# A perceiver block: the probabilities turned on VectorE, the mix of four heads in row quarters, PSUM banks in turn

## The chip, the cores and the metric

The kernel runs on one core of a Trainium2 chip. The metric is the device time of one execution in microseconds (us). Engines are TensorE (PE in the profile, its weight loads PEld), VectorE (DVE), ScalarE (ACT), GpSimd (POOL) and SyncE (SP), which only issues DMAs here. All data are 32-bit floats.

## The reference

Sixty-four sequences of 32 tokens, 256 wide, go through three residual layers: attention to a context, attention within the sequence, and a mixture of experts. The change touches the first.

```python
# xattn: 16 heads of 64; q [64, 32, 256], kv [64, 257, 128]
qh = (q @ Wq).reshape(B, N, 16, 64).transpose(0, 2, 1, 3)
kh = (kv @ Wk).reshape(B, M, 16, 64).transpose(0, 2, 1, 3)
vh = (kv @ Wv).reshape(B, M, 16, 64).transpose(0, 2, 1, 3)
attn = softmax(einsum("bhnd,bhmd->bhnm", qh, kh) * 64 ** -0.5)
out = einsum("bhnm,bhmd->bhnd", attn, vh).transpose(0, 2, 1, 3).reshape(B, N, 1024)
out = out @ Wo + bo
...
x = x + xattn(layernorm(x), ctx_512)      # ctx_512: [64, 257, 128]
x = x + attn(layernorm(x))                # 4 heads of 64, 32 tokens, rotary angles
x = x + ffn(layernorm(x))                 # 8 experts, the best 2 of each token
```

## The kernel before, in words

**Tiling.** A tile is 128 tokens, so four sequences; there are 16 tiles, and 64 sequences in the loop `for n, (t, b) in enumerate(seqs)`. The key and value weights are folded: the queries are multiplied by the key weights once (`cross_queries`, for two tiles at a time), and the scores are then products with the raw context; the mix of the raw context by the probabilities comes next (`cross_mix`), and the value and output weights after it (`cross_output`).

**One sequence.** `cross_probs` works in four groups of four heads, so that the 128 partitions are 4 heads x 32 tokens. For a group it makes the scores of 257 context rows (L315, one PSUM bank), the negated maximum on VectorE (L319), and the exponential with its sum on ScalarE (L320); after every second group VectorE takes the reciprocals (L325) and scales both groups' first 256 probabilities (L327). The 257th context row goes another way (`p_last`, `lastT`, `u_last`). `probs_transposed` turns the probabilities in two halves of 128 context rows: four TensorE transposes into one bank (L338) and one ScalarE copy (L342). `cross_mix` multiplies the two halves with the context's rows, two products of 128 rows by 512 columns (16 heads x 32 tokens) that add up in one bank (L348), and ScalarE copies it to `cT` (L351).

**Order.** The instruction order of TensorE and SP is the program's own; a scheduler orders the other engines. In the loop's pass `n`, the mix of sequence `n` and the scores of sequence `n + 1` are woven with steps of three more strands, which a table `steps` names for each pass: `near` and `far` are the rests of the last two tiles (`rest`: output of the cross attention, self attention, routing), and `ahead` is the queries of a pair of tiles to come. Before the change a pass is

```python
probs_transposed(t, b, 0, pr, pts)
step()
next(scores, None)
next(scores, None)
step()
probs_transposed(t, b, 1, pr, pts)
nc.vector.transpose(lastT[:, b, :], p_last[t % 2][b])
next(scores, None)
step()
next(scores, None)
step()
step()
cross_mix(t, b, pts, kvs[t][1], cT)
step()
```

**PSUM.** The eight banks stand in three rings: three for the scores (tag `s`), two for transposes (`t`), three for all else (`a`). A ring's next tile waits until the tile that it takes the place of has been read.

**Names in the profile.** L291 `pqh` and L270 `pq` are the queries (L270 on the two halves of TensorE's rows in turn), L298 the scaling that evicts `pqh`, L281 and L283 the copies that evict `pq`; L364 `pov` is the value product (two column halves), with L374 (VectorE) and L372 (ScalarE) as its two evictions, L377 and L381 the output product, L386 its residual add; L197 transposes for other stages and L198 evicts them, L396 is the self attention's q/k/v product, L399 adds its bias, L426 its scores (two row halves by four column strips), L442 its exponential, L451 its small transposes, L456 its mix; L483 and L527 belong to the routing, L183 to the layer norms (a power on GpSimd), L1076 is the transpose of `p_last`. L712 and L745 are the experts' products, L684 a VectorE transpose there. After the loop the experts run in blocks of 128 rows with weights that SP loads into three lanes.

Of the kernel before, what the change touches and what calls it, by code (L numbers as in the profile page):

```python
# [24 lines left out]
MC = 2  # L25
ML = MC * P
# [24 lines left out]
def block_kernel(  # L51
# [29 lines left out]
    ps = ctx.enter_context(tc.tile_pool(name="ps", bufs=3, space=PSUM))  # L81
# [37 lines left out]
    def load_context(t):  # L119
        kv = kvp.tile([P, W1LEN], FP, tag="kv", name=f"kv{t}")  # L120
        kvT = kv[:, : 4 * M].rearrange("p (b m) -> p b m", b=4)
        kvA = kv[:, 4 * M : 4 * M + 4 * ML].rearrange("p (b c d) -> p b c d", b=4, c=MC)
        load(kvT, ctx_t[:, 4 * t : 4 * t + 4, :])
        load(kvA, ctx_a[:, 4 * t : 4 * t + 4, :, :])
        return kvT, kvA
# [11 lines left out]
    load(xwo_sb, xwo.rearrange("(c p) k -> p c k", p=P))  # L137
    for t in range(2, 4):
        load_tokens(t)
# [30 lines left out]
    def bank(shape, name):  # L170
        return ps.tile([P] + shape, FP, tag="a", name=name)
# [17 lines left out]
    def transposed(dst, src, n, name, beside=False):  # L189


        if beside:
            pt = ps.tile([P, n, P], FP, tag="t", bufs=2, name=f"tr{name}")
        else:
            pt = bank([n, P], f"tr{name}")
        for k in range(n):
            nc.tensor.transpose(pt[:, k, :], src[:, k * P : (k + 1) * P], ident)  # L197
        nc.scalar.copy(dst, pt)  # L198
# [5 lines left out]
    def last_rows():  # L204
        v_last = wk.tile([P, XH // 2, NB], FP, tag="v_last", bufs=1, name="v_last")
        pv = bank([XH // 2, NB], "pv")
# [10 lines left out]
        for half in range(2):  # L217
            pu = [bank([2, D], f"pu{half}_{par}") for par in range(2)]
# [31 lines left out]
    def cross_queries(c):  # L250
# [5 lines left out]
        for j in range(2):  # L256
            transposed(xqT[:, :, j * P : (j + 1) * P], xns[j], 2, f"q{2 * c + j}")


        qh = wk.tile([P, XH // 2, 2 * P], FP, tag="qh", bufs=1, name=f"qh{c}")  # L260
# [3 lines left out]
        def of_heads(i):  # L264
            pq = [bank([2, 8, SEQ], f"pq{c}_{i}_{par}") for par in range(2)]
# [19 lines left out]
        for i in range(4):  # L285
            yield
            pq = bank([2, 2 * P], f"pqh{c}_{i}")
# [17 lines left out]
    def cross_probs(t, b, kvT):  # L305
# [6 lines left out]
        probs[t, b] = pr  # L312
        for g in range(4):
            s = ps.tile([P, M], FP, tag="s", name=f"s{t}_{b}_{g}")
# [8 lines left out]
            if g % 2:  # L323
                two = slice(g - 1, g + 1)
                nc.vector.reciprocal(inv[:, two], sums[:, two])  # L325
                for i in (g - 1, g):
                    nc.vector.tensor_scalar(  # L327
                        pr[:, i, :ML], pr[:, i, :ML], inv[:, i : i + 1], None, ALU.mult
                    )
# [5 lines left out]
    def probs_transposed(t, b, j, pr, pts):  # L335
        tp = ps.tile([P, 4 * P], FP, tag="t", bufs=2, name=f"tp{t}_{b}_{j}")
        for g in range(4):
            nc.tensor.transpose(  # L338
                tp[:, g * P : (g + 1) * P], pr[:, g, j * P : (j + 1) * P], ident
            )  # L340
        pt = ptp.tile([P, 4 * P], FP, tag=f"pt{j}", name=f"pt{t}_{b}_{j}")
        nc.scalar.copy(pt, tp)  # L342
        pts.append(pt)

    def cross_mix(t, b, pts, kvA, cT):
        pa = bank([4 * P], f"pa{t}_{b}")
        for j in range(MC):
            nc.tensor.matmul(  # L348
                pa, kvA[:, b, j, :], pts[j], start=(j == 0), stop=(j == MC - 1)
            )  # L350
        nc.scalar.copy(cT[:, :, b, :], pa.rearrange("p (h n) -> p h n", n=SEQ))  # L351

    def cross_output(t, cT, lastT, ut):
# [4 lines left out]
        for half in range(2):  # L358
            pv = bank([4, P], f"pov{t}_{half}")
# [16 lines left out]
        po = bank([D], f"po{t}")  # L376
# [3 lines left out]
        for m in range(XH // 2):  # L380
# [3 lines left out]
            if m == 3:  # L384
                yield
        nc.vector.tensor_tensor(xs[t], po, xb, ALU.add)  # L386

    def self_attention(t, xn):
        xaT = wk.tile([P, 2, P], FP, tag="xaT", name=f"xaT{t}")
        transposed(xaT, xn, 2, f"s{t}", t < NT - 2)  # L390
        yield
        qkv = wk.tile([P, 3 * D], FP, tag="qkv", name=f"qkv{t}")
        for lo, hi in ((0, 512), (512, 768)):
            pq = bank([hi - lo], f"pqkv{t}_{lo}")
# [20 lines left out]
        transposed(qkT, qkv, 4, f"qk{t}")  # L415
# [831 lines left out]
```

## Time and profile before

| what | value |
|---|---|
| median of 3 runs (lowest to highest) | 807.62 us (801.75 to 809.26) |
| the profiled execution: its time, its span | 802.53 us, 800.8 us |
| granted TensorE clock | 0.993 |
| PE / PEld busy | 771.7 / 604.5 us |
| VectorE / ScalarE / GpSimd busy | 503.1 / 365.3 / 152.4 us |
| moved by DMA | 64.17 MB, mean 80 GB/s |
| VectorE's scaling of the probabilities, L327 | 256 of 353 ns, 79.7 us |
| TensorE's transposes of them, L338 | 512 of 279 ns, 80.5 us busy |
| their evictions on ScalarE, L342 | 128 of 591 ns, 75.6 us |
| the mix, L348 | 256 instructions of 604 ns, 123.2 us busy |

Durations are those of single instructions, from start to modelled end; TensorE's instructions overlap, so a mean of 604 ns does not say that the next one starts 604 ns later. The distance between starts is read from the timeline. Each f32 product appears as two instructions.

### The profile page before, as it was taken

How to read it: one execution, taken by the hardware profiler on the slowest of the kernel's cores; microseconds unless marked ns; L12 is line 12 of the kernel's file. 1: busy time of each engine (PE TensorE's matmuls, PEld its weight loads, DVE VectorE, ACT ScalarE, POOL GpSimd, SP SyncE). 2: the span in 40 equal slices, each digit the busy share in tenths (PEclk: the TensorE clock that was granted, in tenths of full speed). 3: DMA queues.
4: the chain of work that ended last, by engine and by line, in shares of the span. 5: the costliest groups of instructions: out<-in, count | busy, mean ns of one | idle time of the engine just before them, and what ended most of it. 6: DMA issues, size and time to landing. Idle time of an engine off the chain costs nothing. (4 is left out here: it accounts for less than half of the span.)

```text
span 800.8 us, 15293 instructions
## 1 busy us (share of the span) xinstructions
PE 771.7 (96%) x5146; PEld 604.5 (75%) x5146; DVE 503.1 (63%) x2084; ACT 365.3 (46%) x1052; POOL 152.4 (19%) x214
## 2 busy tenths in 40 slices
PE   8899999999999999999999999999999899999994
PEld 7576677677767777777767777676678799999994
DVE  4657666766686676677677766768665633554442
ACT  3564555555465555546554555555434222212220
POOL 3001011120211111111111111121124412332332
PEclk9999999999999999999999999999999999999997
DMA  9440102021120202021110202020351396458432
GB/s 309 142 111 2 67 11 68 11 89 27 53 73 18 67 11 80 11 69 50 50 60 18 68 11 67 10 78 15 119 203 34 80 398 180 54 110 251 58 45 28
DMA packets 44258, 64.17 MB, mean 80 GB/s; under 512 B 19408, under 2 KB 35152, under 8 KB 42640
## 3 DMA queue, kind: packets, MB, share of 16 engines
q1 hardware_dynamic: 37648, 54.08, 20.8%
q0 software_dynamic: 6528, 9.06, 6.2%
q8 instruction: 43, 0.70, 0.4%
q14 instruction: 39, 0.32, 0.1%
HBM read 87.54 MB, written 13.16 MB: 126 GB/s over the span
## 5 line engine op out<-in xcount | busy, mean ns | idle before, releaser
L320 ACT ACTIVATE pr<-s,nmx 128x257 f32<-128x257 f32 x256 | 122.2, 481 | 111.8 <-DVE nmx L319 100.5
L319 DVE TENSOR_REDUCE nmx<-s 128x1 f32<-128x257 f32 x256 | 105.4, 420 | 71.0 <-PE s L315 70.4
L315 PE MATMUL s<-kv,q 128*128 128x257 f32 x512 | 143.1, 388 | 1.9 <-ACT pr L320 1.9
L348 PE MATMUL pa<-pt,kv 128*128 128x512 f32 x256 | 123.2, 604 | 5.0 <-ACT ov L372 4.9
L315 PEld LDWEIGHTS s<-kv,q 128*128 128x128 f32 x512 | 89.3, 193 | 16.7 <-ACT pr L320 3.2
L338 PEld LDWEIGHTS tp<-ident,pr 128*128 128x128 f32 x512 | 61.8, 144 | 30.6 <-issue 15.7
L338 PE MATMUL tp<-ident,pr 128*128 128x128 f32 x512 | 80.5, 279 | 1.6 <-DVE pr L327 1.6
L327 DVE TENSOR_SCALAR pr<-pr,inv 128x256 f32<-128x256 f32 x256 | 79.7, 353 | 3.4
L351 ACT COPY cT<-pa 128x512 f32<-128x512 f32 x64 | 37.5, 586 | 91.4 <-PE pa L348 91.4
L342 ACT COPY pt<-tp 128x512 f32<-128x512 f32 x128 | 75.6, 591 | 4.5 <-PE tp L338 3.5
L348 PEld LDWEIGHTS pa<-pt,kv 128*128 128x128 f32 x256 | 46.1, 190 | 39.4 <-issue 26.6
L752 POOL DMA_INDIRECT out_x<-y_late,to_late x28 | 43.5, 1555 | 104.0 <-DMA out_x<-y_late,to_late 39.0
L291 PE MATMUL pqh<-xqT,xwq_sb 128*128 128x256 f32 x256 | 60.8, 381 | 0.8 <-ACT xqT L198 0.8
L381 PE MATMUL po<-xwo_sb,ov 128*128 128x256 f32 x256 | 60.6, 379 | 0.0
L381 PEld LDWEIGHTS po<-xwo_sb,ov 128*128 128x128 f32 x256 | 48.6, 190 | 6.6
L291 PEld LDWEIGHTS pqh<-xqT,xwq_sb 128*128 128x128 f32 x256 | 47.3, 190 | 7.9 <-ACT xqT L198 1.5
L320 ACT ACTIVATION_READ_ACCUMULATOR pr<-s,nmx 128x1 f32 x256 | 52.1, 203 | 0.0
L325 DVE RECIPROCAL inv<-sums 128x2 f32<-128x2 f32 x128 | 20.8, 162 | 46.7 <-ACT pr L320 45.8
L728 ACT ACTIVATE sa_late<-pa_late,lane 128x128 f32<-128x128 f32 x72 | 20.6, 369 | 63.6 <-PE pa_late L712 63.6
L555 POOL TENSOR_SCALAR carried<-seen,is_last 128x8 f32<-128x8 f32 x15 | 5.3, 353 | 218.6 <-DVE seen L550 218.6
L539 POOL DMA_INDIRECT routed<-xr,rslots x32 | 33.0, 1032 | 59.2 <-DMA routed<-xr,rslots 22.0
L396 PE MATMUL pqkv<-awqkv_sb,xaT 128*128 128x512 f32 (+1 forms) x128 | 43.9, 486 | 0.0
(275 smaller groups left out, 1270.8 us busy)
## 6 DMA issues: line engine op xcount, KB each, us to landing
lane<-in_wall SPq DMA_DIRECT2D x24, 1028.0 KB
lane<-in_wall SPq DMA_DIRECT2D x24, 640.0 KB
lane2a<-in_wall SPq DMA_DIRECT2D x10, 1028.0 KB
kv<-in_ctx_t SPq DMA_DIRECT2D x16, 514.0 KB
kv<-in_ctx_a SPq DMA_DIRECT2D x16, 512.0 KB
lane2b<-in_wall SPq DMA_DIRECT2D x10, 640.0 KB
xg_late<-routed SPq DMA_DIRECT2D x80, 32.0 KB
x<-in_x SPq DMA_DIRECT2D x16, 128.0 KB
```

The costliest lines, as they stand in the source:

```text
L291: nc.tensor.matmul(pq[:, mm, :], xwq_sb[:, k, m * P : (m + 1) * P], xqT[:, k, :], start=(k == 0), stop=(k == 1),)
L315: nc.tensor.matmul(s, qb[:, g * P : (g + 1) * P], kvT[:, b, :], start=True, stop=True)
L319: nc.vector.tensor_reduce(nmx, s, AX.X, ALU.max, negate=True)
L320: nc.scalar.activation(pr[:, g, :], s, AF.Exp, bias=nmx, accum_out=sums[:, g : g + 1])
L327: nc.vector.tensor_scalar(pr[:, i, :ML], pr[:, i, :ML], inv[:, i : i + 1], None, ALU.mult)
L338: nc.tensor.transpose(tp[:, g * P : (g + 1) * P], pr[:, g, j * P : (j + 1) * P], ident)
L342: nc.scalar.copy(pt, tp)
L348: nc.tensor.matmul(pa, kvA[:, b, j, :], pts[j], start=(j == 0), stop=(j == MC - 1))
L351: nc.scalar.copy(cT[:, :, b, :], pa.rearrange("p (h n) -> p h n", n=SEQ))
L381: nc.tensor.matmul(po, ov[:, m, :], xwo_sb[:, m, :], start=False, stop=(m == XH // 2 - 1))
L396: nc.tensor.matmul(pq, xaT[:, k, :], awqkv_sb[:, k, lo:hi], start=(k == 0), stop=(k == 1))
L752: nc.gpsimd.indirect_dma_start(out=out[:, :], out_offset=bass.IndirectOffsetOnAxis(ap=self.to[:, b : b + 1], axis=0), in_=y, in_offset=Non ...
```

## The change

- The scaling of the probabilities moves from VectorE to ScalarE. After every second group VectorE turns the two groups' 256 columns in squares of 32 x 32 (`prT`); TensorE's transposes and their ScalarE copies go.
- A square's transpose stays within its 32 partitions, so that head `h` of each group has its probabilities, turned, in partitions `32 h` to `32 h + 31`. The mix is therefore 8 chunks of 32 context rows x 4 heads of a group: 32 products of 32 rows by 128 columns (4 groups x 32 tokens), each head in its quarter of TensorE's rows and in its bank. One ScalarE copy empties the four banks.
- Each quarter needs the context's rows in its own partitions: the rows of a sequence are loaded four times (`load_values`, three buffers, asked for two sequences ahead), where a tile's were loaded once. The transposed context (`kvT`) keeps its load.
- The eight banks are one tile, and each use takes the bank, or the row of four, whose last use is longest ago; banks that stay open over several steps are held.
- To make room, the rotary tables' small tiles lie in a tile of the routing, the third lane in that of the queries, `v_last` in that of `xqT`, and `sa` and `g` of the experts share one tile. The host lays `ctx_a` out by chunks of 32.

```diff
-MC = 2
-ML = MC * P
+MC = 8
+ML = MC * SEQ
...
-    ps = ctx.enter_context(tc.tile_pool(name="ps", bufs=3, space=PSUM))
+    psum = ctx.enter_context(tc.tile_pool(name="ps", bufs=1, space=PSUM))
+    psum = psum.tile([P, 8, 512], FP, name="psum")
...
     def load_context(t):
-        kv = kvp.tile([P, W1LEN], FP, tag="kv", name=f"kv{t}")
-        kvT = kv[:, : 4 * M].rearrange("p (b m) -> p b m", b=4)
-        kvA = kv[:, 4 * M : 4 * M + 4 * ML].rearrange("p (b c d) -> p b c d", b=4, c=MC)
+        kvT = kvp.tile([P, 4, M], FP, tag="kvT", name=f"kvT{t}")
         load(kvT, ctx_t[:, 4 * t : 4 * t + 4, :])
-        load(kvA, ctx_a[:, 4 * t : 4 * t + 4, :, :])
-        return kvT, kvA
+        return kvT
+
+    def load_values(n):
+
+        kvA = kvp.tile([P, MC, KVD], FP, tag="kvA", bufs=3, name=f"kvA{n}")
+        for h in range(4):
+            load(kvA[h * SEQ : (h + 1) * SEQ, :, :], ctx_a[:, n, :, :])
+        values.append(kvA)
...
     load(xwo_sb, xwo.rearrange("(c p) k -> p c k", p=P))
+    values = []
+    for n in range(2):
+        load_values(n)
...
-    def bank(shape, name):
-        return ps.tile([P] + shape, FP, tag="a", name=name)
+    taken, held = [0] * 8, set()
+
+    def banks(n):
+
+        at = min(
+            (i for i in range(9 - n) if held.isdisjoint(range(i, i + n))),
+            key=lambda i: max(taken[i : i + n]),
+        )
+        taken[at : at + n] = [max(taken) + 1] * n
+        return at
...
+    def bank(shape):
+        return view(banks(1), shape)
+
+    def hold():
+        at = banks(1)
+        held.add(at)
+        return at
...
         pr = pp.tile([P, 4, M], FP, tag="pr", name=f"pr{t}_{b}")
-        probs[t, b] = pr
+        prT = ptp.tile([P, MC, 4, SEQ], FP, tag="pt", name=f"prT{t}_{b}")
+        probs[t, b] = prT
         for g in range(4):
-            s = ps.tile([P, M], FP, tag="s", name=f"s{t}_{b}_{g}")
+            s = bank([M])
...
                 for i in (g - 1, g):
-                    nc.vector.tensor_scalar(
-                        pr[:, i, :ML], pr[:, i, :ML], inv[:, i : i + 1], None, ALU.mult
-                    )
+                    nc.scalar.mul(pr[:, i, :ML], pr[:, i, :ML], inv[:, i : i + 1])
+
+                nc.vector.transpose(
+                    prT[:, :, two, :], pr[:, two, :ML].rearrange("p g (c m) -> p c g m", c=MC)
+                )
...
-    def probs_transposed(t, b, j, pr, pts):
-        tp = ps.tile([P, 4 * P], FP, tag="t", bufs=2, name=f"tp{t}_{b}_{j}")
-        for g in range(4):
-            nc.tensor.transpose(
-                tp[:, g * P : (g + 1) * P], pr[:, g, j * P : (j + 1) * P], ident
-            )
-        pt = ptp.tile([P, 4 * P], FP, tag=f"pt{j}", name=f"pt{t}_{b}_{j}")
-        nc.scalar.copy(pt, tp)
-        pts.append(pt)
-
-    def cross_mix(t, b, pts, kvA, cT):
-        pa = bank([4 * P], f"pa{t}_{b}")
-        for j in range(MC):
-            nc.tensor.matmul(
-                pa, kvA[:, b, j, :], pts[j], start=(j == 0), stop=(j == MC - 1)
-            )
-        nc.scalar.copy(cT[:, :, b, :], pa.rearrange("p (h n) -> p h n", n=SEQ))
+    def cross_mix(n, prT, kvA, cT):
+
+
+        at = banks(4)
+        for c in range(MC):
+            for h in range(4):
+                r = slice(h * SEQ, (h + 1) * SEQ)
+                nc.tensor.matmul(
+                    psum[:, at + h, :P],
+                    kvA[r, c, :],
+                    prT[r, c, :, :].rearrange("p g n -> p (g n)"),
+                    start=(c == 0),
+                    stop=(c == MC - 1),
+                )
+        nc.scalar.copy(
+            cT[:, :, n % 4, :].rearrange("p (g h) n -> p h g n", h=4),
+            psum[:, at : at + 4, :P].rearrange("p h (g n) -> p h g n", n=SEQ),
+        )
...
-        pr, pts = probs.pop((t, b)), []
-        probs_transposed(t, b, 0, pr, pts)
+            scores = cross_probs(t1, b1, kvs[t1])
+        if n + 2 < len(seqs):
+            load_values(n + 2)
         step()
         next(scores, None)
+        step()
         next(scores, None)
+        nc.vector.transpose(lastT[:, b, :], p_last[t % 2][b])
         step()
-        probs_transposed(t, b, 1, pr, pts)
-        nc.vector.transpose(lastT[:, b, :], p_last[t % 2][b])
         next(scores, None)
         step()
         next(scores, None)
         step()
-        step()
-        cross_mix(t, b, pts, kvs[t][1], cT)
+        cross_mix(n, probs.pop((t, b)), values[n], cT)
         step()
```

## The prediction

> **What bounds the kernel now.** I read the page's engine shares first, then a table by stage, then who waited for whom, then the timeline of TensorE in the loop.
>
> ```profile
> PE 771.7 (96%) x5146; PEld 604.5 (75%) x5146; DVE 503.1 (63%) x2084; ACT 365.3 (46%) x1052; POOL 152.4 (19%) x214
> ```
>
> TensorE's share is an average, so the loop over the sequences has to be looked at by itself (columns: window, PE, PEld, DVE, ACT, POOL busy with counts, granted clock, DMA share, GB/s):
>
> ```profile
> 200.00:300.00 100.00, 98.88 (x656) 72.32 (x656) 70.38 (x290) 54.96 (x158) 16.86 (x27) 1.00 0.14 45
> 300.00:400.00 100.00, 98.88 (x648) 72.80 (x647) 69.12 (x281) 54.03 (x157) 16.15 (x26) 1.00 0.16 52
> ```
>
> TensorE is busy 98.9% at full clock; VectorE has 30% idle, ScalarE 45%, the DMA engines 85%. Who held TensorE up, in the whole span (total us, times, longest):
>
> ```profile
> PE pa L348 <- ACT ov L372: 4.9, 13, 0.4
> PE s L315 <- ACT pr L320: 1.9, 3, 1.0
> PE tp L338 <- DVE pr L327: 1.6, 1, 1.6
> ```
>
> So the loop lasts as long as TensorE's own stream. The first mix products (L348) of sequences 4 and 56 start at 61.5 and 526.5 us: 465/52 = 8.94 us a sequence. What a group costs is the distance from its start to the next group's (start, busy, group):
>
> ```profile
> 291.76 0.60 PE L315 MATMUL s<-kv,q 128*128 128x257 f32 x2
> 292.29 1.14 PE L270 MATMUL pq<-qh,xwk_sb 64*128 64x256 f32 x8
> 293.36 0.70 PE L315 MATMUL s<-kv,q 128*128 128x257 f32 x2
> ...
> 302.71 1.88 PE L348 MATMUL pa<-pt,kv 128*128 128x512 f32 x4
> 304.42 0.28 PE L527 MATMUL pk<-rfed,before_all 128*128 128x8 f32 x2
> ...
> 305.07 1.03 PE L315 MATMUL s<-kv,q 128*128 128x257 f32 x4
> 305.94 0.60 PE L197 MATMUL trqk<-ident,qkv 128*128 128x128 f32 x4
> 306.38 0.60 PE L338 MATMUL tp<-ident,pr 128*128 128x128 f32 x4
> ...
> 310.29 0.38 PE L426 MATMUL pss<-qkT 64*32 64x32 f32 x32
> 311.05 1.13 PE L348 MATMUL pa<-pt,kv 128*128 128x512 f32 x2 [0.37 <-ACT ov L372]
> ```
>
> An f32 product is two instructions, a transpose is one. 128 columns step at 0.11 us (306.38 - 305.94 over 4), 257 at 0.217, 512 at 0.43. The reader should see L270: eight instructions of 256 columns on two row halves take 1.07, where one after the other would be 8 x 0.217 = 1.74. The halves run side by side.
>
> **Part by part: TensorE.** Removed for each sequence: 8 transposes x 0.11 = 0.88, and the mix, 304.42 - 302.71 = 1.71. Together 2.59, over 64 sequences 165.8. Added: 32 products of 32 rows x 128 columns, 64 instructions, four quarters taking turns. If four run at once that is 16 steps x 0.11 = 1.76. Entering and leaving a split array costs too: L270 takes 1.07 where four steps are 0.87 (0.20), and the score product ahead of it takes 0.53 and not 0.435 (0.10). So 2.06, over 64 131.8. No row has four row quarters. The bounds are 1.76 (no switch) and 64 x 0.11 + 0.30 = 7.34 (one at a time); two at a time is 32 x 0.11 + 0.30 = 3.82. The nearest rows are L270 (a full two at a time on two halves) and L426 (two halves by four column strips: 32 instructions of 32 columns start within 0.38 - 0.20 = 0.18 us, where single file at 0.027 would be 0.83, so more than four run at once). I take 2.06. Net -33.9.
>
> The first page rule against this: the Trainium skill ("TensorE: Matmul & The Clock Gate", section "Measured speedup vs the span model") measured four row quarters at 3.07 times one, not 4. By it the mix would be an estimated 7.04/3.07 + 0.30 = 2.59, nothing would be won on the products, and the sum below would end at about 811. The trace has pairs only, and those lose nothing but the switch.
>
> The second: the same page ("The mechanism") says that a weight load overlaps running products only where the row group differs. Each quarter here loads new weights for every product. But the full-array mix above loads 0.19 us of weights (L348's PEld row) for each product in a 0.43 step with no gap, on the same rows, so the trace disagrees. With L270's load of 0.186 in the open in each step the mix would be about 5.0, and the sum about 967.
>
> **VectorE and ScalarE.** (line, engine, op, shapes, count, busy us, mean ns, idle before)
>
> ```profile
> L327 DVE TENSOR_SCALAR pr<-pr,inv 128x256 f32<-128x256 f32 x256 | 79.7, 353 | 3.4
> L342 ACT COPY pt<-tp 128x512 f32<-128x512 f32 x128 | 75.6, 591 | 4.5 <-PE tp L338 3.5 <-ACT cT L351 0.2
> ...
> L1076 DVE STREAM_TRANSPOSE lastT<-p_last 128x32 f32<-128x32 f32 x64 | 13.0, 203 | 0.2
> L684 DVE STREAM_TRANSPOSE bxT_late<-xg_late 128x256 f32<-128x256 f32 x20 | 8.7, 435 | 0.0
> L442 ACT ACTIVATE apr<-sc,zero 128x128 f32<-128x128 f32 x16 | 6.4, 401 | 10.8 <-DVE sc L434 10.8
> ```
>
> VectorE loses 256 scalings (79.7) and gets 128 transposes of 512 elements. From 32 to 256 elements costs 232 ns, 1.04 a column, so 435 + 265 = 0.70 each, 89.6: +10. ScalarE loses 75.6 of evictions and gets 256 scalings of 128x256 in SBUF; the rows around are 0.371 (L198's copy, 256 columns), 0.401 (L442, the one that reads SBUF) and 0.481 (L320). I take 0.40: 102, or +27. Per sequence that is +0.15 and +0.41 against idle of 2.8 and 4.1: nothing by the sums. Both orders are fixed queues, though, so the waits matter more.
>
> What is new there: reciprocal (VectorE), two scalings (ScalarE), transpose (VectorE) is a round trip, and VectorE queues later maxima, and with them the exponentials that free score banks, behind the transpose. The mix needs the transposed probabilities one whole sequence later, so it does not wait for them. It waits for banks. In the changed kernel's order the four banks of a mix were mostly last used three or more groups back. In one of four sequences (the one after which a tile ends) the newest of them is the third score's, with one score product (0.435) in between. From the end of the second score: 0.20 to land, max 0.42, exponential with sum 0.63, reciprocal 0.16 = 1.41. In one tile of two, the q/k/v product (2.57) stands between second and third score, so the mix could start at 2.57 + 0.87 = 3.44; VectorE adds the bias (starts at 1.91 when its product has landed, to 2.52), transposes (the scalings ended at 2.26) to about 3.14, adds the other bias to 3.50, takes the third max to 3.92; the exponential ends at about 4.45. Stall 1.0. In the other tile 1.71 stands there, and the mix could start at 2.58; ScalarE's order is scalings to 2.3, eviction of the queries (0.60) to 2.9, third exponential to 3.4. Stall 0.85. Mean 0.93 x 16 = +15. Bounds: 0 if the scheduler's slack is larger than I count, and 45 if every mix waits 0.7, one transpose.
>
> **Banks, memory, loads.** Banks in turn put the mix on banks other than the second L372 eviction's: the 4.9 goes, and with the transposes the 1.6 goes: -6.5. The values come four times over, 512 KB a sequence and not 128, 25 MB more, by four DMAs on SP, asked for two sequences (some 17 us) ahead. The page's first slice moves 309 GB/s, so 512 KB take 1.7 us; SP has only stores and later loads behind that wait. Cost nothing; if this cover went, 1.7 x 64 = 109 would be the most. The first values now come behind the output weights, some 4.5 MB into the stream or 15 us at that rate, still ahead of the first mix (30.1 us). The rotary tables' and third lane's new places cost nothing while their old owner is done well before: the queries' tile is last used some eight sequences earlier. The expert stage keeps its products and two held banks: nothing.
>
> **Sum.** -33.9 + 15 - 6.5 = -25.4 on the profiled execution's 802.5 us (span 800.8): 777.1. That execution stands 0.6% under the median, 807.62, of runs from 801.75 to 809.26. I forecast 777.
>
> **Rivals.**
> - VectorE's queue becomes the bound (the slower side). In the loop:
>
> ```profile
> DVE nmx L319 <- PE s L315: 48.4, 57, 2.1
> DVE inv L325 <- ACT pr L320: 34.3, 57, 0.8
> ```
>
> from 100 to 500 us, 44.7 sequences. Waiting for scores is slack; waiting for exponentials (0.77 a sequence), for GpSimd's powers (0.32) and the small exponential (0.09) is not. VectorE's busy 6.18 + 0.15 + 1.18 = 7.51; two round trips of 0.80 with nothing queued between make 9.11, 0.17 above 8.94: +11, 813. It decides from 1.43 us unfilled on; against it, the order puts a bias add, eviction or residual add in most of the gaps, and half filled leaves 8.3. Chance 0.13.
> - The quarters run two at a time or with loads in the open: 3.82 adds 1.76 x 64 = 113 to the sum: about 890. For it, no row shows four; against it L426. Chance 0.09.
> - Half way: stalls at all mixes (45, not 15) give 807, no change. For it, VectorE is 70% busy and in order. Chance 0.15.
> - No stall at all: 762. For it, the trace before has almost none. Chance 0.10.
> - Forecast: 0.53.
>
> **How the numbers follow.** 1% is what a measurement here tells from no change. Faster (below some 799): forecast, no stall and a part of the half-way case, 0.68. Same: most of the rest of the half-way case, 0.12. Slower: VectorE's queue with its upper neighbours, and the quarters, 0.20. Range: from 757, a little under no stall, to 815, just past VectorE's queue; the quarters' case is left out. The forecast's own range is 762 to 792.
>
> **What would show it.** The mix group at 2.0 to 2.1 us from its start to the next group's (3.8 says two at a time); VectorE's transposes at 0.70; the scalings at 0.40; mix starts 8.5 us apart; TensorE's waits naming the mix behind the third exponential about 15 us in total and in every fourth sequence; VectorE waiting for scores still, though less. I am wrong if VectorE no longer waits for scores, or if the mix takes over 2.6.

## The result

The changed kernel takes 810.41 us (median of 15 runs), the kernel before 804.69 (15 runs): 1.0074 times as long, 95% interval 1.005 to 1.0099. So it is a little slower, where 777 us were forecast. The profiled execution has a span of 809.0 us (before 800.8).

The page's engine shares of the changed kernel:

```profile
PE 766.7 (95%) x8474; PEld 640.0 (79%) x8474; DVE 507.7 (63%) x1956; ACT 406.2 (50%) x1180; POOL 151.6 (19%) x214
```

Two hundred microseconds of its loop by stage (window, PE, PEld, DVE, ACT, POOL busy, granted clock, DMA share, GB/s):

```profile
200.00:300.00 100.00, 98.07 (x1229) 78.35 (x1229) 71.33 (x268) 61.64 (x178) 16.88 (x27) 1.00 0.29 89
300.00:400.00 100.00, 98.07 (x1219) 78.43 (x1218) 69.99 (x257) 61.44 (x179) 16.12 (x26) 1.00 0.32 95
```

TensorE still looks full. A busy share does not show what happened inside: TensorE's groups got shorter, and its waits longer. The groups of the new parts (busy us, mean ns of one, idle time before them):

```profile
L375 PE MATMUL psum<-prT,kvA 32*128 32x128 f32 x4096 | 157.7, 282 | 9.9 <-ACT pr L351 4.8 <-DMA bn_bc<-in_bias_n 1.1 <-DVE qkv L435 1.0
L375 PEld LDWEIGHTS psum<-prT,kvA 32*128 32x128 f32 x4096 | 138.2, 188 | 30.4 <-issue 10.3 <-ACT pr L351 8.5 <-ACT q L311 2.5
L358 ACT ACTIVATE pr<-pr,inv 128x256 f32<-128x256 f32 x256 | 115.7, 502 | 39.5 <-DVE inv L356 37.7 <-issue 1.2
L360 DVE STREAM_TRANSPOSE prT<-pr 128x512 f32<-128x512 f32 x128 | 89.7, 701 | 30.1 <-ACT pr L358 30.0
```

The mix (L375) is 64 instructions in one group. Undisturbed, the first and the last of them start 1.80 us apart (16 steps of four quarters, 0.21 us from the first step to the second and 0.11 from then on), and the next group starts at 2.0. By place in the eight sequences of two tiles (sequences 8 to 55, means in us; the stall is what the distance from first to last start has over 1.80):

| place | 0 | 1 | 2 | 3 | 4 | 5 | 6 | 7 |
|---|---|---|---|---|---|---|---|---|
| mix to next mix, before | 9.92 | 8.58 | 9.93 | 9.00 | 9.92 | 8.12 | 8.22 | 8.24 |
| mix to next mix, after | 9.91 | 8.29 | 9.51 | 9.01 | 9.81 | 8.29 | 8.10 | 8.91 |
| stall inside the mix, after | 0.45 | 0 | 0.21 | 0.74 | 0.34 | 0 | 0.53 | 1.54 |

The stalls come to 3.81 in eight sequences, 30 us in 64. Places 0 and 4 have 0.79 of the 3.81; there the profile names nothing that the mix waits for. TensorE's timeline at the worst place (a place 7, sequence 31):

```profile
301.87 1.03 PE L346 MATMUL psum<-kvT,q 128*128 128x257 f32 x4
302.83 0.49 PE L375 MATMUL psum<-prT,kvA 32*128 32x128 f32 x4
303.51 0.48 PE L375 MATMUL psum<-prT,kvA 32*128 32x128 f32 x2 [0.19 <-DVE qkv L435]
304.44 2.05 PE L375 MATMUL psum<-prT,kvA 32*128 32x128 f32 x58 [0.45 <-ACT pr L351]
306.42 0.39 PE L563 MATMUL psum<-rfed,before_all 128*128 128x8 f32 x2
```

Four of its 64 instructions run, then it waits for a bank that the q/k/v addition (L435) empties, then for one that the third score's exponential (L351) empties: 3.59 us to the next group and not 2.0. VectorE's timeline says why that exponential is late:

```profile
301.30 0.17 DVE L356 RECIPROCAL inv<-sums 128x2 f32<-128x2 f32 x1 [0.76 <-ACT pr L351]
301.38 0.67 DVE L435 TENSOR_TENSOR qkv<-psum,abqkv_bc 128x512 f32<-128x512 f32 x1
302.44 0.71 DVE L360 STREAM_TRANSPOSE prT<-pr 128x512 f32<-128x512 f32 x1 [0.39 <-ACT pr L358]
303.07 0.39 DVE L435 TENSOR_TENSOR qkv<-psum,abqkv_bc 128x256 f32<-128x256 f32 x1
303.38 0.41 DVE L350 TENSOR_REDUCE nmx<-psum 128x1 f32<-128x257 f32 x1
```

The third maximum (L350) stands behind a transpose that waits for ScalarE's scalings. So far the prediction's picture holds. What it does not say is how much of this belongs to the waiting transpose, and how much to the bank that the mix picked.

Where the profiled 8.2 us went: the first mix starts at 27.1 us (before 30.1), the last at 582.7 (580.8), and from there to the end it is 226.3 us (220.0): -3.0, +4.9, +6.3. Over sequences 4 to 56 a sequence takes 8.98 us, before 8.94, and the forecast said 8.5. The loop kept nothing of the saving, and the stage behind it lost more.

### The profile page after: what moved, and what is told of

It is laid out like the page before. It is cut to its first block, busy times and chain, and to the rows that moved or that the text cites. A ratio compares the mean times of both kernels' runs of the same rounds, so it can differ in the third digit from the quotient of the medians.

```text
span 809.0 us, 22230 instructions
## 1 busy us (share of the span) xinstructions
PE 766.7 (95%) x8474; PEld 640.0 (79%) x8474; DVE 507.7 (63%) x1956; ACT 406.2 (50%) x1180; POOL 151.6 (19%) x214
## 5 line engine op out<-in xcount | busy, mean ns | idle before, releaser
L351 ACT ACTIVATE pr<-psum,nmx 128x257 f32<-128x257 f32 x256 | 120.8, 475 | 106.2 <-DVE nmx L350 105.7
L375 PE MATMUL psum<-prT,kvA 32*128 32x128 f32 x4096 | 157.7, 282 | 9.9 <-ACT pr L351 4.8
L375 PEld LDWEIGHTS psum<-prT,kvA 32*128 32x128 f32 x4096 | 138.2, 188 | 30.4 <-issue 10.3
L346 PE MATMUL psum<-kvT,q 128*128 128x257 f32 x512 | 150.3, 394 | 1.0 <-ACT q L311 0.8
L358 ACT ACTIVATE pr<-pr,inv 128x256 f32<-128x256 f32 x256 | 115.7, 502 | 39.5 <-DVE inv L356 37.7
L350 DVE TENSOR_REDUCE nmx<-psum 128x1 f32<-128x257 f32 x256 | 103.0, 413 | 42.3 <-PE psum L346 41.2
L360 DVE STREAM_TRANSPOSE prT<-pr 128x512 f32<-128x512 f32 x128 | 89.7, 701 | 30.1 <-ACT pr L358 30.0
L346 PEld LDWEIGHTS psum<-kvT,q 128*128 128x128 f32 x512 | 87.5, 190 | 22.6 <-issue 9.6
L747 PE MATMUL psum<-bxT_late,lane 128*128 128x128 f32 x576 | 69.1, 275 | 1.2 <-DMA lane<-in_wall 1.2
L747 PEld LDWEIGHTS psum<-bxT_late,lane 128*128 128x128 f32 x576 | 68.1, 192 | 2.3 <-ACT bxT_late L717 1.3
L351 ACT ACTIVATION_READ_ACCUMULATOR pr<-psum,nmx 128x1 f32 x256 | 50.5, 197 | 0.0
L575 POOL DMA_INDIRECT routed<-xr,rslots x32 | 33.0, 1030 | 48.4 <-DVE nmx L350 17.8
```

The source lines that it names most:

```text
L346: nc.tensor.matmul(s, qb[:, g * P : (g + 1) * P], kvT[:, b, :], start=True, stop=True)
L350: nc.vector.tensor_reduce(nmx, s, AX.X, ALU.max, negate=True)
L351: nc.scalar.activation(pr[:, g, :], s, AF.Exp, bias=nmx, accum_out=sums[:, g : g + 1])
L358: nc.scalar.mul(pr[:, i, :ML], pr[:, i, :ML], inv[:, i : i + 1])
L360: nc.vector.transpose(prT[:, :, two, :], pr[:, two, :ML].rearrange("p g (c m) -> p c g m", c=MC))
L375: nc.tensor.matmul(psum[:, at + h, :P], kvA[r, c, :], prT[r, c, :, :].rearrange("p g n -> p (g n)"), start=(c == 0), stop=(c == MC - 1),)
```

## The experiments

All ratios are against the kernel before, with 95% intervals. "First to last mix" is from the profile, to tell the loop from the stage behind it.

**The scaling back on VectorE.**

```diff
-                    nc.scalar.mul(pr[:, i, :ML], pr[:, i, :ML], inv[:, i : i + 1])
+                    nc.vector.tensor_scalar(
+                        pr[:, i, :ML], pr[:, i, :ML], inv[:, i : i + 1], None, ALU.mult
+                    )
```

> The scaling of the probabilities goes back to VectorE, all else stays as changed. Theory A (the round trip from VectorE to ScalarE and back sits in VectorE's fixed order, makes the third maximum and ScalarE's evictions late, and the mixes wait for their banks): the wait of VectorE for the scalings (19.7 us from 100 to 500 us) goes, but two scalings of some 0.27 us each stand in its place ahead of the same third maximum, about as long as the two on ScalarE (0.91) less the hop; so little changes, 800 to 815 us. Rival B (VectorE's load as such is the bound of the loop): 4 x 0.27 = 1.1 us more a sequence, 64 x 1.1 = 70, about 870 us at the most and over 830 us at the least.

Measured 831.57 us, 1.0355 (1.0326 to 1.0384). 21 us above the changed kernel: too much for theory A. It lies at the lower edge of what rival B allowed (over 830), with a third of its 70. It is not spread evenly: at place 7 it is 11.23 us from mix to next mix, 2.32 more than in the changed kernel, and over all eight places 3.07 more. So VectorE's work isn't the bound everywhere, but where it is late already, more of it is paid.

**Half of the mix left out.**

```diff
-        for c in range(MC):
+        for c in range(MC // 2):
...
-                    stop=(c == MC - 1),
+                    stop=(c == MC // 2 - 1),
```

> The mix takes only the first four of its eight chunks of context rows, so half of the mix is left out; loads, transposes and scalings stay. It asks whether TensorE's stream is still what the loop lasts as long as. Theory A (TensorE's stream with waits inside it): eight steps of 0.11 us less a sequence, 64 x 0.88 = 56, so about 755 us, or some 770 us if part of it turns into longer waits for banks. Rival B (VectorE, ScalarE or a chain through them sets the pace of a sequence): the shorter mix is filled by waits, 795 to 810 us.

Measured 788.79 us, 0.9838 (0.9804 to 0.9873). The last mix starts at 565.1 us, 17.6 earlier, for 56 us of products left out. Neither theory as stated: TensorE's stream still matters, but less than a third of a saving gets through. At place 7 the halved mix still takes 3.11 us where it could take 0.90.

**Scalings and transposes in the next pass.** They are taken out of the groups' loop, kept for the next pass and pinned there (`keep_in_program_order`, here `pin`: behind what its engine was given before).

```diff
+        turn = turns.pop((t, b))
         step()
         next(scores, None)
+        scaled(turn, 0)            # pin(ScalarE: both scalings of a pair)
         step()
         next(scores, None)
         nc.vector.transpose(lastT[:, b, :], p_last[t % 2][b])
+        turned(turn, 0)            # pin(VectorE: the pair's transpose)
+        scaled(turn, 2)
         step()
         next(scores, None)
+        turned(turn, 2)
```

> The scalings and the transposes of a sequence are put off into the next pass, and pinned there: the first pair's scalings behind the first exponential of the next sequence on ScalarE and its transpose behind the second maximum on VectorE, the second pair's a group later. The same work, but nobody waits for a round trip any more: reciprocals are long done, scalings stand a group ahead of their transpose, and the mix is still half a pass away. Theory A: VectorE's waits for the scalings (19.7 us) go, the third maxima come earlier, and of the 29 us that mixes stand in the middle most go: 780 to 790 us. Rival B (the load of VectorE and ScalarE, or what TensorE pays for entering and leaving the split array, is the cause): no more than 5 us either way, 805 to 815 us.

A miss: 834.89 us, 1.0383 (1.0344 to 1.0421). Who waited for whom from 100 to 500 us:

```profile
PEld psum L388 <- DVE prT L376: 28.7, 32, 1.8
DVE prT L376 <- ACT pr L369: 23.3, 33, 1.2
```

The mixes (L388 here) now wait for the transposes (L376 here) themselves. The edit gave away the lead of nearly a whole sequence that the changed kernel has, and so tested something else.

**Banks 4 to 7 for the mix alone.**

```diff
+        if apart[0] and n == 4:
+            return 4
...
-            (i for i in range(9 - n) if held.isdisjoint(range(i, i + n))),
+            (i for i in range((4 if apart[0] else 8) + 1 - n) if held.isdisjoint(range(i, i + n))),
```

> While the loop runs (up to its last four passes), the mix has banks 4 to 7 for itself, and all other groups take turns in banks 0 to 3. A mix then waits only for the copy of the mix before, some 7 us back. Theory A in its narrow form (the mix's four banks are what waits, and nothing else is late): the 29 us of stalls inside the mixes go and a ring of four is deep enough for the rest, about 782 us. Theory A in its wide form (the maxima and exponentials are late, whoever waits for them): the waits move to the scores and to the products of the other strands, which now find their bank after four groups instead of some eight, 800 to 830 us. Rival B (loads, supply of instructions or engine load): no change, 805 to 815 us.

Measured 825.91 us, 1.0286 (1.0258 to 1.0315). Every mix now takes 1.80 us from first to last start, so with banks of its own it has no stall left. That would fit waits for banks at every place; for places 0 and 4 the run with three sequences' values, below, shows something else at work. And the loop is longer (9.22 us a sequence): the other groups wait instead in their ring of four. The wide form of theory A.

**One group earlier** (the edit is against the run with the next pass). The first pair's scalings stand at the head of the pass, its transpose behind the first maximum.

```diff
+        scaled(turn, 0)
         step()
         next(scores, None)
-        scaled(turn, 0)
+        turned(turn, 0)
+        scaled(turn, 2)
         step()
         next(scores, None)
+        turned(turn, 2)
         nc.vector.transpose(lastT[:, b, :], p_last[t % 2][b])
-        turned(turn, 0)
-        scaled(turn, 2)
         step()
         next(scores, None)
-        turned(turn, 2)
```

> As the run before with scalings and transposes in the next pass, but one group earlier each: the first pair's scalings at the head of the pass, its transpose behind the first maximum, the second pair's scalings behind the first exponential, its transpose behind the second maximum. There the mixes had turned to wait for the transposes (VectorE's second transpose was 28.7 us of TensorE's waits from 100 to 500 us). Theory A (the round trip inside a pass makes the third maximum late, and the mixes wait for banks): neither wait is left, VectorE's waits for scalings are under 5 us, and the loop comes to some 8.5 us a sequence: 780 to 790 us. Rival B (load): the lead gained is spent on other waits, and it stays at 805 to 830 us.

Measured 811.39 us, 1.0100 (1.0068 to 1.0132): no gain in time, against theory A. Sequences 4 to 56 take 8.83 us each, 0.15 less than in the changed kernel or 7.8 us together, but from mix 56 to the last mix it is 66.0 us and not 56.7: the last mix alone waits 5.4 us for its transposes, which stand behind a tile's routing here. So the total says little about the loop. In the loop the mixes at places 3 and 7 still stall, 0.84 and 1.02 us, though VectorE waits for no scaling there any more. So the waiting transpose is not what holds the mix.

**The scalings left out.**

```diff
-                for i in (g - 1, g):
-                    nc.scalar.mul(pr[:, i, :ML], pr[:, i, :ML], inv[:, i : i + 1])
```

> The scalings are left out (the mix gets unnormalised probabilities), all else as changed; a transpose then waits for its exponentials alone. ScalarE loses 4 x 0.41 = 1.64 us a sequence, and the way from the second exponential of a pair to the end of the transpose gets shorter by 0.16 for the reciprocal and 0.91 for the scalings. Theory A: the stalls inside the mixes (0.46 us a sequence) fall to a third or less and the waits ahead of other groups go too: 775 to 787 us. Rival B with ScalarE's load as the bound would give the same sign. Rival C (what TensorE pays for switching, the supply of its many instructions, or the order of its own stream costs the gain): nothing changes, 805 to 815 us.

Measured 815.75 us, 1.0144 (1.0091 to 1.0196). The unnormalised values send the tokens to other experts, and behind the last mix it takes 245.2 us, so only the loop can be read: 8.85 us a sequence, stalls of 0.73 and 1.27 at places 3 and 7. Even with no scaling in the kernel the stalls stay. Theory A as I had it falls here.

**The kernel before, with its scalings on ScalarE.**

```diff
-                    nc.vector.tensor_scalar(
-                        pr[:, i, :ML], pr[:, i, :ML], inv[:, i : i + 1], None, ALU.mult
-                    )
+                    nc.scalar.mul(pr[:, i, :ML], pr[:, i, :ML], inv[:, i : i + 1])
```

> The kernel before with one part alone: the 256 scalings on ScalarE in place of VectorE; TensorE's transposes, their copies, the three rings of banks and the loads stay. VectorE loses 4 x 0.27 = 1.1 us a sequence, ScalarE gains 4 x 0.41 = 1.64. Theory A (it is the round trip together with VectorE's transpose that hurts): without a VectorE transpose nothing on VectorE waits for the scalings but the products with the 257th column do not need them either, TensorE's transposes come a sequence later, so no change: 798 to 808 us. Rival B (ScalarE's share of evictions and exponentials is late as soon as scalings stand ahead of them): the score banks come free later, up to 0.9 us once or twice a sequence, 820 us and more.

Measured 823.08 us, 1.0239 (1.0183 to 1.0296): rival B. In the kernel before, with its three rings, this one part of the change costs some 19 us by itself. From mix to mix, 2.54 of the 2.75 us that eight sequences lose stand between the last mix of a tile and the first of the next. ScalarE's and TensorE's timelines where a tile begins:

```profile
317.90 0.93 ACT L327 ACTIVATE pr<-pr,inv 128x256 f32<-128x256 f32 x2
318.70 0.66 ACT L198 COPY xqT<-trq 128x256 f32<-128x256 f32 x2
319.14 1.09 PE L362 MATMUL pov<-cT,xwv_sb 128*64 128x128 f32 x16 [0.41 <-ACT xqT L198]
320.06 0.91 ACT L327 ACTIVATE pr<-pr,inv 128x256 f32<-128x256 f32 x2 [0.23 <-DVE inv L325]
320.87 0.56 ACT L370 COPY ov<-pov 128x512 f32<-128x512 f32 x1
321.18 1.10 PE L346 MATMUL pa<-pt,kv 128*128 128x512 f32 x2 [0.63 <-PE pss L424]
```

Two scalings stand ahead of the copy of `xqT`, and the value product waits 0.41 us for its bank; two more stand ahead of the copy of `ov`, and the mix starts 0.63 us late. The profile names L424 as its releaser, which had long been done. ScalarE is far from full, but it takes its instructions one after another in their order, and here 0.9 us of work that nobody waits for yet stands ahead of an eviction for which TensorE waits.

**A held bank counts as used when it is let go.**

```diff
-        held.remove(at)
+        release(at)                # held.remove(at); taken[at] = max(taken) + 1
...
-            held.difference_update(self.banks.pop(b))
+            release(*self.banks.pop(b))
```

> The changed kernel with one line of its turn of the banks changed: a bank that is held over several steps counts as used last when it is let go, not when it was taken. As changed, the next group takes just such a bank as the one longest unused and waits for its eviction: in the profile after, TensorE waits 1.70 and 1.52 us for the experts' gated product behind the loop, where the kernel before has no such wait. Expected: those two waits (3.2 us) go, and in the loop the bank of the output product is no longer taken at once after its release; 804 to 808 us. Rival (the 6.3 us behind the last mix come from VectorE's order and late gathers): no change, 808 to 812 us.

Measured 809.57 us, 1.0076 (1.0053 to 1.0099). From the last mix to the end it takes 225.0 us and not 226.3. In the changed kernel TensorE's waits behind the loop include these two:

```profile
PE psum L226 <- DVE sag_early L769: 1.7, 1, 1.7
PE psum L611 <- DVE sag_early L769: 1.5, 1, 1.5
```

Both are gone with the edit, but the experts' second product waits in their place (1.5 us for the same gated product), a wait that the kernel before has too. Those 6.3 us are for the most part something else.

**The row of four set aside ahead of the mix.** The alternatives so far changed when banks come free. This one changes only which are taken. As changed, the mix must find four neighbours when it comes. At places 3 and 7 every such row holds the third score's bank, which was used two groups back.

```diff
+            if not kept and 9 <= p < 60:      # p: mixes so far
+                if singles[p % 8] - since[1] <= ahead_of_mix[p % 4]:   # (4, 2, 2, 2)
+                    kept.append(oldest_row())
...
-            (i for i in range(9 - n) if held.isdisjoint(range(i, i + n))),
+            (i for i in range(8) if i not in held and not (kept and kept[0] <= i < kept[0] + 4)),
```

> The changed kernel with the same instructions in the same order on TensorE, and only other banks: a few groups ahead of each mix (four in the sequence that begins a tile, two in the others) the row of four whose use is longest ago is set aside, and the groups until the mix take turns in the other four. As changed, a row of four neighbours must be found when the mix comes, and in the last sequence of each tile it always holds the third score's bank, used two groups back; now the newest bank of a row was used four or more groups back. Theory D (the earlier theory A has fallen, since neither putting the scalings off nor leaving them out took the stalls away: it is the row of four banks next to each other that makes the mix wait for the newest score's exponential): the stalls of those sequences (0.74 and 1.54 us) go, 8 x 2.28 = 18 us, and some 6 more in the first sequences of tiles: 786 to 793 us. Theory E (the strands' own chains through VectorE and ScalarE take about 9 us a sequence at these places of the order, so that a wait taken from the mix comes back at the next score or transpose): 803 to 812 us.

Measured 806.56 us, 1.0029 (1.0003 to 1.0056). TensorE's timeline at the same place 7:

```profile
302.69 2.07 PE L395 MATMUL psum<-prT,kvA 32*128 32x128 f32 x64
304.69 0.39 PE L583 MATMUL psum<-rfed,before_all 128*128 128x8 f32 x2
...
306.88 0.66 PE L246 MATMUL psum<-ident,xnq 128*128 128x128 f32 x4 [0.40 <-ACT cT L402]
```

All 64 instructions in one piece: theory D is right on what the mix waited for (places 2, 3 and 7 have no stall left). And theory E is right on the time: 4 us and not 18 to 24, since waits come back elsewhere: at transposes, at the self attention's scores, inside the mix at place 4 (0.34 is now 0.56).

**Three edits together** (the scalings one group earlier, rows set aside, release).

> The three edits together: the scalings and transposes in the next pass, half a pass ahead of the mix (a loop of 8.83 us a sequence was measured with it, 8.98 without), the rows of four set aside ahead of each mix, and held banks counted as used when they are let go. Theory D: the 18 to 24 us of the set-aside rows come on top of the 52 x 0.15 = 8 us of the loop: 775 to 788 us, faster than the kernel before. Theory E: the waits come back elsewhere, 800 to 812 us.

Measured 800.13 us, 0.9952 (0.9923 to 0.9982): faster than both kernels, but not yet what theory D asked. The first two alone gave 0.15 and 0.05 us a sequence; the three together 0.31.

**One group earlier still, and the first row earlier.** In the last run TensorE's weight loads still waited 4.4 us (from 130 to 490 us) for late transposes, all ahead of the mixes at places 3 and 7, and the mixes at places 0 and 6 still stalled 0.52 and 0.83 us. The edit is against the three together.

```diff
+        scaled(turns[t, b], 0)     # behind the fourth exponential, same pass
+        turned(turns[t, b], 0)
...
-        scaled(turn, 0)
+        scaled(turn, 2)
         step()
         next(scores, None)
-        turned(turn, 0)
-        scaled(turn, 2)
+        turned(turn, 2)
         step()
         next(scores, None)
-        turned(turn, 2)
```

and `ahead_of_mix` is `(5, 2, 2, 2)`.

> The three edits together once more, with the scalings and transposes one group earlier still (the first pair's behind the fourth exponential of the same pass, the second pair's scalings at the head of the next pass and its transpose behind the first maximum there), and the row of four set aside five groups ahead in the sequence that begins a tile. With the three edits TensorE still waited from 130 to 490 us for transposed probabilities (4.4 us, all in the third sequence of tiles) and for the newest evictions in the first sequences (5.3 us); both should go, 64/41 x 9 = some 14 us over the loop at the most. Theory D with both causes named (late transposes, and rows of four used too lately): 786 to 796 us. Theory E (something else late comes up each time a wait is taken away): 797 to 806 us.

Measured **787.19 us, 0.9805 (0.9769 to 0.9840)**, the fastest kernel with the whole computation. The loop takes 8.56 us a sequence, and at no place do the mixes stall over 0.04 us on the mean. (Behind mix 56 the last mix still waits 5.3 us for its second transpose.) By stage, and the two groups that had waited for each other:

```profile
300.00:400.00 100.00, 98.81 (x1209) 79.20 (x1209) 74.23 (x270) 64.02 (x185) 15.14 (x25) 1.00 0.34 96
```

```profile
L396 ACT ACTIVATE pr<-pr,inv 128x256 f32<-128x256 f32 x256 | 115.4, 501 | 0.0
L403 DVE STREAM_TRANSPOSE prT<-pr 128x512 f32<-128x512 f32 x128 | 90.5, 707 | 6.7 <-ACT pr L396 6.2
```

The same instructions at nearly the same durations as in the changed kernel, with the same number of products and the same loads, so neither the split array nor the instruction count kept the changed kernel at 8.98 us; idle before the scalings 39.5 is 0.0, before the transposes 30.1 is 6.7.

**Values loaded for three sequences only.**

```diff
+        if n >= 3:
+            values.append(values[n - 3])
+            return
         kvA = kvp.tile([P, MC, KVD], FP, tag="kvA", bufs=3, name=f"kvA{n}")
```

> The changed kernel with the context's rows loaded for the first three sequences only and used again for all others (so the mix of 61 sequences uses the wrong rows), which leaves out some 32 MB of loads. If the fourfold loads cost nothing in the loop, as the prediction has it: 806 to 813 us. If they take something from the loop, from the first mix or from the gathers behind the loop: up to 6 us less, 800 to 806 us.

The whole, 820.21 us, 1.0213 (1.0167 to 1.0259), can't be read, since the wrong values change the experts' share as before (241.9 us behind the last mix). The loop can: first to last mix 548.9 us against 555.6, and only places 0 and 4 change (9.91 and 9.81 to 9.46, their stalls to 0). So the loads do cost the changed kernel some 6 us, at the places where a tile begins, though no bank was changed here. In the 787 us kernel, with all the loads, these mixes don't stall either, so it is not their bandwidth as such. What it is, is open.

**The placing alone** (the 787 us kernel without rows set aside and without release).

> The placing of the scalings and transposes as in the run before (787 us), without the set-aside rows and without the later release. If both causes are real and cover for each other: the mixes wait for their rows again (1.8 us grows to 2.3 or more in the first and last sequences of tiles), 795 to 806 us. If the placing alone was the cause: 786 to 791 us. If the rows alone were: 805 us and more.

Measured 801.74 us, 0.9975 (0.9940 to 1.0010). At places 3 and 7 the mixes stall again, 0.73 each:

```profile
293.21 0.50 PE L390 MATMUL psum<-prT,kvA 32*128 32x128 f32 x6
293.97 2.05 PE L390 MATMUL psum<-prT,kvA 32*128 32x128 f32 x58 [0.26 <-ACT pr L351]
```

**Half of the mix left out once more**, now from the 787 us kernel, with the same edit as above.

> The kernel of 787 us with half of the mix left out (four chunks of eight), as was done to the changed kernel, where the 64th mix came 17.6 us earlier for 56 us of products left out. The wrong values change which experts the tokens go to, so the loop is to be read (first mix to 64th mix), not the end. If TensorE's stream is again what the loop lasts as long as: the 64th mix comes at 510 to 525 us instead of 562.7. If VectorE's and ScalarE's chains are only just behind it: 530 to 550 us.

Measured 760.74 us, 0.9466 (0.9410 to 0.9521), last mix at 536.7 us: 26 of 56 us get through, where the changed kernel let 17.6. The loop gets 0.40 us a sequence shorter where 0.88 was taken out, and at places 1, 5 and 7 the distance to the next mix doesn't shrink at all. So TensorE's stream sets the pace of this kernel at most places, and the other engines' chains are only some 0.4 us a sequence behind it.

The two causes, in us a sequence (sequences 4 to 56):

| | row found when the mix comes | row set aside ahead |
|---|---|---|
| scalings and transposes as changed | 8.98 | 8.93 |
| in the next pass, the earlier placing | 8.73 | 8.56 |

The last cell has the later release too, which alone changed nothing in the loop (8.99), and the first row set aside one group earlier.

## Why the prediction was wrong, point by point

**Right: the products.** The mix takes 2.0 us to the next group, and the group ahead of it takes up to 0.10 longer than elsewhere (0.96 for four score instructions, not 0.87), 0.07 on the mean: 2.07 where 2.06 was forecast. TensorE's own work is 0.52 us a sequence less, as forecast (0.53). The four quarters do run at once: 64 instructions of 0.11 us would be 7.04 one after another, and the group takes 2.0, 3.5 times as fast; from the second step on, four start every 0.11, the time of one. The Trainium skill ("TensorE: Matmul & The Clock Gate", section "Measured speedup vs the span model") has 3.07 for four row quarters of 512 columns; for the 128 columns here the measurement decides. Its section "The mechanism" says that a load overlaps running products only where the row group differs (or, as it says further up, where it goes to a background weight buffer), and by the first of these each load would stand in the open after a product on the same rows; the loads (188 ns each, so 3.0 us for each quarter's 16) lie beside the products of their own quarter, since the whole group takes 2.0. VectorE's transpose (0.701, forecast 0.70) and the two removed waits (6.5 us) were right too.

**Wrong in size: the stalls.** This is the step that failed most. "Mean 0.93 x 16 = +15" became 30. In the loop the forecast stands for 8.54 us a sequence: 8.94, less 0.53 for the products, plus 0.23 of stalls, less 0.10 for removed waits. Measured is 8.98: 8.94, less 0.52, plus 0.48 of stalls, plus 0.08 of other waits. So the stalls are 0.25 of the 0.44 us that a sequence is over the forecast, and waits ahead of other groups, which were put at nothing, are 0.18. The main place was right: the mix that ends a tile, behind the third exponential. Its even tile was 0.74 (forecast 0.85), its odd one 1.54 (1.0); and the first and third sequences of a tile, which were put at nothing, had 0.21 to 0.53, or 12 of the 30 us. The step counted "the four banks of a mix were mostly last used three or more groups back" and took it for given that at the fourth place a score's bank is among them. It wasn't asked why. The bank is there because the four must be neighbours, which a kernel can arrange beforehand.

**Wrong in kind: "nothing by the sums".** The prediction set ScalarE's +0.41 and VectorE's +0.15 a sequence against idle time and took only the mixes' stalls for what queues cost. The kernel before with its scalings moved shows what such a sum leaves out: about 19 us with VectorE's work smaller and nothing else changed, through evictions that stand behind 0.91 us of scalings. The figure belongs to that kernel and its rings. How much of the changed kernel's loss is this term, no run shows: without any scaling its loop gained only 0.13 us a sequence, while the stalls at places 3 and 7 stayed. The forecast needed, for each eviction on TensorE's way, what stands ahead of it in its queue.

**Not priced: the covers.** There are two causes, late scalings and transposes and a row of banks that is found late, and each is in part hidden by the other. Against the changed kernel, the better placing alone gave 9 us (811 us and none in its first form), the rows alone 4, and both with the later release 23. The prediction's loop of 8.54 us a sequence nearly came out (8.56) once both were gone, but that is luck: the forecast counts 0.23 of stalls inside the mixes, of which next to nothing is left there, and other waits make up for them.

**Costed at nothing, and not nothing.** The values' loads: some 6 us, at places 0 and 4 (a part of the 30 above). The stage behind the last mix: 6.3 us more in the profile. Other turns of the banks alone give 225.0 and 222.9 there, the 787 us kernel 221.8, so some of it seems to be banks that are taken too soon; the rest is not settled. On the other side the first mix came 3.0 us earlier, which wasn't forecast either. ScalarE's scalings were 0.50 and not 0.40, two of them in 0.91, which at the path's places is 0.1 us more each time.

**The rivals.** "Half way" had the time (807) and a part of its reason: stalls at six places of eight, 30 us and not 45. VectorE's queue as the bound (813) had nearly the same time, and it is refuted: without any scaling, so without the round trip, the loop gains only 0.13 us a sequence, and the 787 us kernel has the same work on VectorE in 8.56. The sign "VectorE no longer waits for scores" did not come: it waits 28.8 us for them from 100 to 500 us (before 48.4). Nor did the other, a mix of over 2.6: undisturbed it takes 2.0. TensorE's share of 95%, before 96%, could not tell either.

## What to carry to other kernels

When a change takes work from a full engine and gives it to engines with idle time, list for each eviction that the full engine waits for what will stand ahead of it in its queue; the shares of busy time don't tell. Work without a near deadline is best pinned to where its inputs are long there and its reader is still far, and four buffers that must lie side by side are best set aside before they are needed. If taking away one wait changes nothing, take away two before the theory is dropped: here an edit against one cause alone was worth 0 to 9 us, and both, with the later release, 23.

## What the runs showed of the hardware

- Four row quarters with 128 columns, each with new weights for every product, take one 0.11 us step for all four (1.80 us from the first start to the last of 16 steps), and the next group starts 0.2 us after the last instruction's start.
- A scaling of 128x256 from SBUF to SBUF takes ScalarE 0.50 us (0.91 for two). A square transpose of 128x512 takes VectorE 0.70.
- The Trainium skill ("TensorEngine Tiling (Array Packing)", section "Gotcha 1: PSUM Pressure") says that row tiles need different PSUM banks and can't use one at the same time. No run here tried them in one bank; what the runs add is the price of four at once out of eight: 1.54 us a mix at the worst place where the row was found late, on the mean at most 0.04 at any place in the 787 us kernel.
